# A four-layer scan, FFT and attention kernel: sums moved into PSUM, PSUM banks asked for one at a time, and background steps ordered by the due times of the scan

## The chip, the cores and the metric

The kernel runs on one core of one Trainium2 chip. Its time is the device time of one launch in microseconds (us), and the median of several runs is given. One more execution was recorded by the hardware profiler, with every instruction of the five engines and every DMA. PE is the matrix engine, DVE the vector engine, ACT the scalar engine, POOL the GpSimd engine, and SP the engine that issues all DMAs here. PEld is the loading of matmul weights.

## The reference, cut to what matters

Four images of 96 channels and 64 x 64 pixels (L = 4096 tokens) go through four layers. Nearly all of the time is the first layer's selective scan, in four directions k with 192 channels and 16 states each:

```python
# layer 0, for each image b: LN, projection to xi and z, depthwise 3x3 conv, SiLU
xs = stack of xi in 4 orders: rows, columns, both reversed      # [b, 4, 192, L]
dts_r, Bs, Cs = split(einsum('bkdl,kcd->bkcl', xs, x_proj_w))   # 6 + 16 + 16 rows
dt = softplus(einsum('bkrl,kdr->bkdl', dts_r, dt_projs_w) + dt_bias)
h[t] = h[t-1] * exp(dt[t] * A) + dt[t] * B[t] * x[t]            # 16 states per channel
y[t] = sum over the 16 states of h[t] * C[t]
y = y + Ds * xs
ysum = the 4 directions' y, put back in row order and added     # [b, 192, L]
t = x + (layernorm(ysum) * silu(z)) @ out_proj.T
x = t + gelu(layernorm(t) @ mlp_w1.T + b1) @ mlp_w2.T + b2
# layer 1: x + scale * out_proj(layernorm(scan in 2 directions, 1 state) * silu(z)), on group-normed x
# layer 2: x + FFT filter over the tokens; x + FFN quantized to 8-bit floats
# layer 3: x + linear attention (no softmax); x + FFN quantized in the same way
```

## The kernel before

**The scan as a stream of 1536 units.** The foreground is layer 0's scan. A step g is one image, one direction and one quarter of the tokens (4 x 4 x 4 = 64 steps). A step has 24 units, and a unit is 32 channels x 4 states on the 128 partitions by 1024 tokens. Unit i needs four operations: on ACT the *decay* h = exp(dt * A) into one of two PSUM tiles (`decays`, L1438), on POOL the *source* w = u * bb, with u = dt * x (`sources`, L1459), on DVE the scan itself and then the product w = h * cc with C (`recurs`, L1470). PE then sums the 4 states of two units with the matrix `sel` into the PSUM tile `py` (`gathers`, L1504). For every twelfth unit the product with C is made on POOL instead (`side`, L1495). The decay of unit i waits until the product of unit i-2 has freed its PSUM tile. When `py` holds a block (32 x 2 x 2 rows by 512 tokens, eight units), `collects` (L1525) takes it out: for k = 0 ACT copies it to Y in SBUF, for the other directions ACT copies it to `yt` and POOL adds `yt` to Y.

**Preludes.** Before each step, `preludes` (L1340) loads xi, makes xd, dt and u with matmuls, ACT and POOL, and stores dt and u to DRAM. `loads_du` and `loads_bc` bring them back, spread over the partitions.

**Background.** All the rest runs beside the scan: `front` (LN, projection, conv, L438) of the images 1 to 3, then `rest` of each image: `tail` (L609: `gate` adds the D term, normalizes and gates; `group` makes the projection, the MLP and the residuals), `l1`, `l2_front`, `l2_middle`, `back` with `ffn` (L1060). `front` of image 0 comes before the scan. What is left of image 3's `rest` comes after the last scan, with mode `wide`: more workers, five more PSUM banks, and POOL's share of that work on DVE.

**Who sets the order.** The order on each engine is written by a planner when the program is built (`Work`, L62). Every piece of work is a Python generator that yields `on(engine, events, banks, took, table)` before each step. The planner keeps a clock for each engine and takes, again and again, the step that could start first (`choose`, L153). A step's `ready` is 0.25 us after the end of what it needs. A step that would need a change of the activation table is ranked 0.8 us later. A background step on ACT is passed over if the next decay is ready while it would run, save for its last 1.0 us (`LEAD`):

```python
if lead is not None and t is not self.lead and s < lead < s + took - self.LEAD:
    continue
```

Only the thread that asks first may take PSUM banks, and it waits until all of them are free. On the chip every engine then runs its own list strictly in that order and waits on semaphores, so the planned times matter only through the order. Most lines of the profile name a helper: L212 is every matmul, L216 every ACT copy, L227 every ACT activation, L239 every DVE and POOL operation, L260 loads, L264 stores. So operations are told apart by their tiles.

Of the kernel before, what the change touches and what calls it, by code (L numbers as in the profile page):

```python
# [34 lines left out]
    ("l1cb", 1), ("l1A", 2), ("l1D", 2), ("l1og", 1), ("l1ob", 1), ("l1sc", 1),  # L35
# [14 lines left out]
def on(engine, *events, banks=0, took=0.7, table=None):  # L50

    return engine, events, banks, took, table
# [9 lines left out]
class Work:  # L62
# [3 lines left out]
    LEAD = 1.0  # L66

    def __init__(self):
        self.at = dict(pe=0.0, act=0.0, dve=0.0, pool=0.0, sp=0.0)
        self.link = 0.0  # L70
        self.live, self.events, self.free = [], {}, {}
        self.me = self.lead = self.table = None
        self.pools = {}
        self.held = {}

# [68 lines left out]
    def ready(self, t):  # L144
        r = t.end + (self.GAP if t.ask[0] else 0.0)
        for k in t.ask[1]:
            e = k() if callable(k) else self.events.get(k)
            if e is None:
                return None
            r = max(r, e + self.GAP)  # L150
        return r

    def choose(self):  # L153
        lead = self.ready(self.lead) if self.lead and not self.lead.done else None
        first, cands = None, []
        for t in self.live:
            r = self.ready(t)
            if r is None:
                continue
            cands.append((r, t))  # L160
            if t.ask[2] and (first is None or r < first[0]):
                first = r, t
        best = None
        for r, t in cands:
            e, _, n, took, table = t.ask
            if n:
                if t is not first[1] or len(self.free) < n:
                    continue
                r = max(r, sorted(self.free.values())[n - 1])
            s = max(r, self.at[e]) if e else r  # L170
            key = s
            if e == "act":
                if table and table != self.table:
                    key += 0.8
                if lead is not None and t is not self.lead and s < lead < s + took - self.LEAD:
                    continue
            if best is None or (key, t.rank) < best[0]:
                best = (key, t.rank), s, t
        return best
# [22 lines left out]
def tile_hybrid(ctx: ExitStack, tc: tile.TileContext, I: dict, out: bass.AP):  # L202
# [98 lines left out]
    eye = load_const("eye", [C, C])  # L301
# [10 lines left out]
    def setup():  # L312
# [6 lines left out]
        for j in range(3):  # L319
            ve.reduce_sum(dsum[:, j : j + 1], V("Ds", j=4 * j, n=4), axis=mybir.AxisListType.X)  # L320
        ve.reduce_sum(dsum[0:C, 3:4], V("l1D", C, n=2), axis=mybir.AxisListType.X)
# [7 lines left out]
    centd = const.tile([C, C], F32, name="centd")  # L329

# [4 lines left out]
    PREP = 1262  # L335
# [102 lines left out]
    def front(b):  # L438
# [102 lines left out]
        for part in (1, 0):  # L541
# [6 lines left out]
            def conv(q):  # L548
                def job(t):
                    xi = wt(wk, 128, "xi", t)  # L550
                    early = b == 0 and (t == 0 if part else q < 2)
                    if early:
                        yield from taps(xi, xp, 8 * q, V("cw", j=9 * part, n=9))
                        pc = xi
                    else:
                        (pc,) = yield on("pe", banks=1)
# [52 lines left out]
    def tail(b, stat):  # L609
# [12 lines left out]
        def gate(c):  # L622
            y = ys[c]

            def job(t):
                s3 = wt(wk, 128, "s3", t, (3, HC))
                yield on("sp")
                load_packed(s3, xi_d[b][0], c)
                yield on("act", took=2.1)
                for j in range(3):  # L630
                    act(s3[:, j], s3[:, j], AF.Copy, scale=dsum[:, j : j + 1])
# [4 lines left out]
                e2, name = spare()  # L636
                yield on(name)
                e2.tensor_add(y, y, s3)
# [28 lines left out]
        def group(g):  # L667
# [3 lines left out]
            def job(t):  # L671
# [15 lines left out]
                ps = yield on("pe", banks=3)  # L687
                for f in range(3):
                    mm(ps[f], lhsT=m1[:, f * 128 : f * 128 + 128], rhs=hn, start=True, stop=True)
                yield on("act", took=2.2, table=AF.Gelu)  # L690
                for f in range(3):
                    act(s3[:, f], ps[f], AF.Gelu, bias=bias[:, f : f + 1])
                drop(*ps)
                (po,) = yield on("pe", banks=1)
                for f in range(3):
                    mm(po[0:C], lhsT=m2[:, f], rhs=s3[:, f], start=(f == 0), stop=(f == 2))
                yield on("dve")
                ve.scalar_tensor_tensor(x, po[0:C], V("mb2", C), x, ALU.add, ALU.add)
                ve.bn_stats(stat[:, g, :], x)
                drop(po)  # L700
# [14 lines left out]
    def l1_weights(wp):  # L715
        yield on("sp")
        gavg, w_in, w_out = parcel(wp, "rl1", I["r_l1"], 0, [(C, C), (C, DI), (C, C)])
        (dtc,) = parcel(wp, "pl1", prep, 387, [(C + 1, 2 * (C + 4))])
        return gavg, w_in, w_out, dtc.rearrange("p (k c) -> p k c", k=2)

    def l1(b, stat, pp, big):
# [37 lines left out]
        def edges():  # L759
# [5 lines left out]
            po_.memset(big[C : C + 1], 1.0)  # L765
            po_.memset(u[C : C + 1], 1.0)
# [66 lines left out]
        def piece(n):  # L833
# [4 lines left out]
            def job(t):  # L838
# [59 lines left out]
                pc, pv = yield on("pe", banks=2)  # L898
# [3 lines left out]
                yield on("act")  # L902
                act(a, pc[0:C], AF.Square)
                yield on("pe")
# [3 lines left out]
                rstd(a, pv[0:C])  # L908
                drop(pv)
                yield on("dve")  # L910
                ve.scalar_tensor_tensor(a, pc[0:C], V("l1og", C), a, ALU.mult, ALU.mult)
                drop(pc)
# [3 lines left out]
                mm(po[0:C], lhsT=w_out, rhs=a, start=True, stop=True)  # L916
                yield on("dve")
                ve.scalar_tensor_tensor(x, po[0:C], V("l1sc", C), x, ALU.mult, ALU.add)
# [13 lines left out]
    def l2f_weights(wp):  # L932
        yield on("sp")
        mf1, rij, imp = parcel(wp, "rl2", I["r_l2f"], 0, [(128, 128), (128, DI), (128, DI)])
        (w1,) = parcel(wp, "pl2", prep, 587, [(C + 1, DI)])
# [124 lines left out]
    def ffn(x, rs, buf, lay, wk, t):  # L1060
# [5 lines left out]
        pc, pv = yield on("pe", banks=2)  # L1066
        mm(pc[0:C], lhsT=cent, rhs=x, start=True, stop=True)
        yield on("act")
        act(rs, pc[0:C], AF.Square)
        yield on("pe")  # L1070
        mm(pv[0:C], lhsT=avg, rhs=rs, start=True, stop=True)
        yield on("act", took=1.4, table=LN_EXP)
        rstd(rs, pv[0:C])
        drop(pv)
        yield on("dve")
        ve.tensor_tensor(xq, pc[0:C], rs, ALU.mult, saturate=False)
        drop(pc)
# [32 lines left out]
    def back_weights(wp):  # L1110
        yield on("sp")
        mi2, wff, mask = parcel(wp, "rbk", I["r_back"], 0, [(128, 64), (C, C), (C, C)])
        w2, wqt, wkv, vb = parcel(wp, "pbk", prep, 779, [(C, 2 * C), (C, C + 1), (C + 1, 2 * C), (C, 2)])
        return w2.rearrange("p (h c) -> p h c", h=2), vb, mi2, wqt, wkv, wff, mask

    def back(b):
# [4 lines left out]
        yield on("pool")  # L1121
        po_.memset(y0[C : C + 1], 1.0)
# [109 lines left out]
    def prepare():  # L1232
# [5 lines left out]
        w1 = o[0 : C + 1, 587:779]  # L1238
        w2 = o[0:C, 779:971].rearrange("p (h c) -> p h c", h=2)
        wqt, wkv, vb = o[0:C, 971:1068], o[0 : C + 1, 1068:1260], o[0:C, 1260:1262]  # L1240
# [4 lines left out]
        wq = wp.tile([C, C], F32, name="wq")  # L1245
# [15 lines left out]
        get(wq, I["l3_wq"])  # L1261
        (pb,) = yield on("pe", banks=1)
# [18 lines left out]
        yield on("dve")  # L1281
        ve.tensor_mul(sc, sc, bn[:, 0, :])
# [57 lines left out]
    def preludes():  # L1340
        ck, dp = fg["ck"], fg["dp"]
        for g, (b, k, s, c) in enumerate(steps):
# [40 lines left out]
            act(dtu[:, 0], dtu[:, 0], AF.Ln, bias=one)  # L1383
            yield on("pool")
# [53 lines left out]
    def decays():  # L1438
        for i in range(NU + 2):
            if i >= 2:  # L1440
                yield on("act", ("scan" if (i - 2) % SIDE == SIDE - 1 else "C", i - 2), *([("dt", 6 * place(i)[0] + 2 * place(i)[1] + place(i)[3])] if i < NU else []), took=1.3, table=LN_EXP)
# [7 lines left out]
            else:  # L1449
                g, j, q, p, n = place(i)  # L1450
                yield on("act", ("dt", 6 * g + 2 * j + p), took=1.3, table=LN_EXP)
# [7 lines left out]
    def sources():  # L1459
        for i in range(NU):  # L1460
# [4 lines left out]
            yield on("pool", *need)  # L1465
# [4 lines left out]
    def recurs():  # L1470
        for i in range(NU):
# [5 lines left out]
            yield on("dve", *need)  # L1477
            if i % UNITS == 0 and s == 0:
# [25 lines left out]
    def gathers():  # L1504

        for i in range(1, NU, 2):
            g, j, q, p, n = place(i)
            block = 3 * g + j
            yield on("pe", ("C", i), *([("py", block - 1)] if q == 0 and block else []))
            if q == 0:  # L1510
                live["py"] = fg["py"].tile([128, HC], F32, tag="py", name="py")
            for p in range(2):
                w = live["w"].pop(i - 1 + p)
                for f in range(2):
                    r = p * 64 + f * 32
                    o = live["py"][r : r + 32]
                    if steps[g][1] % 2:
# [4 lines left out]
                    mm(o, lhsT=sel4, rhs=v, start=(q == 0), stop=(q == 3))  # L1522
            post("g", i // 2)

    def collects():  # L1525

        for block in range(3 * NS_):
            g, j = divmod(block, 3)
            b, k, s, c = steps[g]
            yield on("act", ("g", 4 * block + 3), took=1.3)  # L1530
            py = live["py"]
            if k == 0 and s == 0 and j == 0:
                live["Y"] = fg["yp"].tile([128, 3, 2048], F32, tag="Y", name="Y")
            Y = live["Y"]
            if k % 2:
                yv = Y[:, j].rearrange("p (r w) -> p r w", w=WW)[:, :, 16 * c : 16 * c + 16]
            else:
                yv = Y[:, j, c * HC : (c + 1) * HC]
            if k == 0:
                copy(yv, py)  # L1540
                post("py", block)
            else:
                t = fg["ck"].tile([128, HC], F32, tag="yt", name="yt", bufs=1)
                copy(t, py)
                post("py", block)
                o = yv
                if k == 2 and straight(b, c):
                    yield on("pool", ("tail", b))
                    o = last["y"][:, j]
                else:  # L1550
                    yield on("pool")
                po_.tensor_add(o, yv, t.rearrange("p (r w) -> p r w", w=16) if k % 2 else t)
# [3 lines left out]
            elif j == 2 and k == 2:  # L1556
                yield on("sp")
                cs = slice(c * HC, (c + 1) * HC)
                put(y_d[b][:, :, cs], Y[:, :, cs])
# [11 lines left out]
    with tc.manual_schedule():  # L1571
# [15 lines left out]
        ts = [wk_.add(f(), 0) for f in (preludes, collects, gathers, side, sources)]  # L1587
# [28 lines left out]
def _constants():  # L1616
# [12 lines left out]
    for k1 in range(64):  # L1629
# [11 lines left out]
        sel4=np.repeat(np.eye(32), 4, axis=0), eye=np.eye(C),  # L1641
# [4 lines left out]
def _layout(a):  # L1646
# [39 lines left out]
    put("l1og", q["out_norm_w"]); put("l1ob", q["out_norm_b"]); put("l1sc", q["scale_w"].reshape(C))  # L1686
# [46 lines left out]
    def packed_columns(*parts):  # L1733
# [12 lines left out]
        r_l1=packed_columns(k["c_gavg"], d.pop("l1_inT"), d.pop("l1_outT")),  # L1746
# [25 lines left out]
```

## Time and profile before

| what | value |
|---|---|
| three runs | 6716.26, 6720.3, 6737.51 us; median 6720.3 |
| profiled execution: time, span | 6725.84 us, 6724.1 us |
| before the first scan | 0 to 142.7 us |
| from the first scan's start to the last scan's end | 142.7 to 6171.0 us, 6028.3 us long |
| in it, busy: DVE, POOL, PE, ACT | 5579.2, 4972.1, 4528.7, 3896.1 us |
| after the last scan | 6171.0 to 6724.1 us, 553.1 us long |
| in it, busy: PE, ACT, DVE, POOL | 429.7, 273.7, 212.6, 14.9 us |
| granted PE clock: before, during, after the scan | 0.96, 0.84, 0.82 |
| ACT table loads | 239 of 1283 ns |
| POOL: adds of `yt` to Y | 141 + 3, 186.5 us |
| POOL: adds of the D term in `gate` | 30, 103.1 us |
| POOL: fills of single rows with 1.0 | 12, 43.0 us |

Read it like this: the time is the sum of three stretches that follow each other. In the middle one, which is nine tenths of the whole, DVE has 5579 us of work and 449 us without work. The page's own chain of work that ended last reaches back over the last stretch and a few pieces before it, and so it says little on the middle one; that has to be read from the waits of DVE.

### The profile page before, as it was taken

What the parts mean: (1) busy time and instruction counts of PE and PEld (TensorE: products, weight loads), DVE (VectorE), ACT (ScalarE), POOL (GpSimd) and SP (SyncE); (2) the same over time, 40 slices, a digit from 0 to 9 for tenths busy, and PEclk for the clock granted to TensorE, in tenths of its full rate; (3) what the DMA queues carried; (4) which work ended last, traced back from release to release, by engine and by line L of the source; (5) the groups of instructions that cost most, each with busy time, mean ns of one, the idle gap of its engine ahead of it and who ended that gap; (6) DMA issues with size and microseconds to landing.
All of it is one profiled execution on the core that took longest, in us unless ns stands there. A gap on an engine that the chain in (4) does not pass through costs nothing. (4 is left out here: it accounts for less than half of the span.)

```text
span 6724.1 us, 54939 instructions
## 1 busy us (share of the span) xinstructions
PE 5070.8 (75%) x15240; PEld 1576.7 (23%) x15240; DVE 5827.8 (87%) x3933; ACT 4222.9 (63%) x6376; POOL 5010.5 (75%) x2319
## 2 busy tenths in 40 slices
PE   7687878766866888767767888767866888767788
PEld 2121212111211332211211232212211332212263
DVE  3899899899999999989989999999999999987613
ACT  3566566555765567766665567876765557765535
POOL 2788788888798788887798788888798778885000
PEclk9688999777868998877879899878877999878788
DMA  4556565656555775555555685566554685562551
GB/s 147 175 173 195 154 202 169 187 173 183 165 183 153 225 265 172 168 169 175 179 172 159 192 295 176 167 189 185 165 184 151 207 283 161 161 178 91 154 158 34
DMA packets 530050, 1188.80 MB, mean 177 GB/s; under 512 B 87970, under 2 KB 161135, under 8 KB 529744
## 3 DMA queue, kind: packets, MB, share of 16 engines
q1 hardware_dynamic: 529744, 1185.30, 57.1%
q8 instruction: 121, 1.98, 0.1%
q14 instruction: 185, 1.52, 0.1%
HBM read 937.50 MB, written 247.59 MB: 176 GB/s over the span
## 5 line engine op out<-in xcount | busy, mean ns | idle before, releaser
L239 POOL TENSOR_TENSOR w<-u,bb 128x1024 f32<-128x1024 f32 x1536 | 3617.0, 2376 | 849.3 <-PE py L212 741.7
L239 DVE TENSOR_TENSOR_SCAN h<-h,state,w 128x1024 f32<-128x1024 f32 x1056 | 2480.2, 2349 | 173.5 <-ACT h L227 112.0
L212 PE MATMUL py<-w,sel 128*32 128x512 f32 x6144 | 1823.9, 971 | 710.1 <-DVE w L239 524.7
L227 ACT ACTIVATE h<-dt,negA 128x1024 f32<-128x1024 f32 x1536 | 1728.6, 1126 | 431.0 <-DVE w L239 309.9
L239 DVE TENSOR_TENSOR w<-h,cc 128x1024 f32<-128x1024 f32 x1408 | 1722.2, 1223 | 107.7 <-DVE h L239 2.7
L239 DVE TENSOR_TENSOR_SCAN h<-h,w 128x1024 f32<-128x1024 f32 x352 | 805.1, 2287 | 103.6 <-ACT h L227 93.7
L216 ACT COPY state<-h 128x1 f32<-128x1 f32 x1056 | 165.8, 157 | 858.7 <-DVE w L239 855.5
L212 PEld LDWEIGHTS py<-w,sel 128*32 128x32 f32 x6144 | 184.8, 117 | 1793.7 <-DVE w L239 1017.7
L239 POOL TENSOR_TENSOR w<-w,cc 128x1024 f32<-128x1024 f32 x128 | 301.3, 2354 | 89.5 <-ACT state L216 53.4
L212 PE MATMUL bm<-xp,dg 128*128 128x512 f32 x792 | 362.3, 605 | 1.3 <-ACT xi L227 1.0
L212 PE MATMUL bm<-xi,xw 128*128 128x512 f32 x384 | 237.6, 769 | 145.6 <-DMA xi<-xi_d 137.1
L227 ACT ACTIVATE dtu<-bm 128x512 f32<-128x512 f32 x384 | 209.4, 600 | 79.2 <-PE bm L212 76.5
L239 POOL TENSOR_TENSOR dtu<-dtu 128x1536 f32<-128x1536 f32 x64 | 221.4, 3459 | 47.6 <-ACT state L216 30.9
L212 PE MATMUL bm<-xd,dtw 64*128 64x512 f32 x384 | 226.2, 675 | 32.2 <-ACT xd L227 5.7
L239 DVE TENSOR_TENSOR_SCAN w<-h,state,w 128x1024 f32<-128x1024 f32 x96 | 224.7, 2341 | 6.4 <-ACT state L216 4.4
L239 POOL MEMSET y<- 1x4096 f32 x4 | 14.1, 3513 | 289.8 <-DMA g_d<-o 289.6
L239 POOL TENSOR_TENSOR dtu<-dtu,xi 128x1536 f32<-128x1536 f32 x64 | 222.5, 3477 | 0.2
L212 PE MATMUL bm<-big,dg 96*96 96x512 f32 x450 | 214.8, 624 | 5.1 <-ACT u L227 3.5
L239 POOL TENSOR_TENSOR Y<-Y,yt 128x512 f32<-128x512 f32 x141 | 182.7, 1296 | 33.2 <-ACT yt L216 21.4
L212 PEld LDWEIGHTS bm<-xp,dg 128*128 128x128 f32 x792 | 145.1, 190 | 263.0 <-issue 248.4
L212 PE MATMUL bm<-x,cent 96*96 96x512 f32 x272 | 158.1, 680 | 53.1 <-DMA x<-in_x 18.5
L239 DVE TENSOR_TENSOR h<-bm,rs 96x512 fp8e5<-96x512 f32 x54 | 36.7, 679 | 162.2 <-ACT rs L227 155.2
(310 smaller groups left out, 7049.5 us busy)
## 6 DMA issues: line engine op xcount, KB each, us to landing
u<-dd SPq DMA_DIRECT2D x384, 512.0 KB
dt<-dd SPq DMA_DIRECT2D x384, 512.0 KB
bb<-bc SPq DMA_DIRECT2D x256, 512.0 KB
cc<-bc SPq DMA_DIRECT2D x256, 512.0 KB
dd<-dtu SPq DMA_DIRECT2D x256, 384.0 KB
xi<-xi_d SPq DMA_DIRECT2D x256, 192.0 KB
f_d<-fo SPq DMA_DIRECT2D x64, 384.0 KB
a<-f_d SPq DMA_DIRECT2D x64, 384.0 KB
```

The lines of the kernel that those rows point to most:

```text
L212: return nc.tensor.matmul(o, lhsT=lhsT, rhs=rhs, **kw)
L216: return nc.scalar.copy(o, i, **kw)
L227: return nc.scalar.activation(o, i, func, **kw)
L239: return f(o, *a, **kw)
```

## The change

The diff has four parts.

**Sums in PSUM.** `gathers` starts each block of `py` with a full 128 x 128 matmul: for k = 0 the D term, from the raw conv output `xj` and the matrix `diagD` (the sum of the four directions' D on the diagonal), for the other directions the part of Y so far, with a unit matrix. ACT then copies `py` straight to Y; `yt` and POOL's adds are gone. A new thread `convolved` loads `xj` for the 48 blocks with k = 0 (four DMAs each). `gate` loses its load of xi, three ACT scalings and the add. In the MLP (`group`) and in layer 1 (`piece`) the residual enters by a unit matrix, and ACT instead of DVE takes the sum out; layer 1's scale is multiplied into its weights beforehand.

**Single-bank requests.** Where a step asked for two or three banks, it asks for one. For that, centred values are copied by ACT from PSUM to SBUF (`dt` in layer 1, `xc` in `ffn`), the reciprocal deviation stays in PSUM, and the MLP's three results are taken out one by one with the bias and go through one Gelu of 1536 columns.

**Due times.** A step of the scan on ACT or POOL carries its unit's number. The planner keeps the pace of the scan and works out by when the unit is due. Until then the step may be ranked up to 0.8 us later, and the next decay blocks background on ACT only from its due time on. A change of table counts with 1.28 us for each load, there and back. Two steps of one thread on the same engine no longer have 0.25 us between them.

**Smaller edits.** Rows of ones come by DMA instead of POOL's fills. In the first image, six of the eight conv pieces of the last part wait until the first prelude has got to its logarithm (`begun`).

```diff
 class Work:
+    UNIT, MARGIN, YIELD, AGE = 3.6, 0.5, 0.8, 0
+    def latest(self, unit, took):
+        i, t = self.pace
+        return t + (unit - i) * self.UNIT - took - self.MARGIN
...
     def ready(self, t):
-        r = t.end + (self.GAP if t.ask[0] else 0.0)
+        r = t.end + (self.GAP if t.ask[0] and t.ask[0] != t.last else 0.0)
...
     def choose(self):
+        if lead is not None and self.lead.ask[5] is not None:
+            lead = max(lead, self.latest(self.lead.ask[5], self.lead.ask[3]))
...
+            if unit is not None:
+                key = max(s, min(s + self.YIELD, self.latest(unit, took)))
             if e == "act":
-                if table and table != self.table:
-                    key += 0.8
-                if lead is not None and t is not self.lead and s < lead < s + took - self.LEAD:
+                if table:
+                    took += 1.28 * ((table != self.table) + (table != LN_EXP))
+                if lead is not None and t is not self.lead and s < lead < s + took - self.LEAD - self.AGE * (s - r):
                     continue
...
     def front(b):
+                    if b == 0 and part == 0 and q >= 2:
+                        yield on(None, ("begun",))
...
         def gate(c):
-                load_packed(s3, xi_d[b][0], c)
-                yield on("act", took=2.1)
-                for j in range(3):
-                    act(s3[:, j], s3[:, j], AF.Copy, scale=dsum[:, j : j + 1])
...
-                e2.tensor_add(y, y, s3)
...
         def group(g):
-                ps = yield on("pe", banks=3)
                 for f in range(3):
-                    mm(ps[f], lhsT=m1[:, f * 128 : f * 128 + 128], rhs=hn, start=True, stop=True)
-                yield on("act", took=2.2, table=AF.Gelu)
-                for f in range(3):
-                    act(s3[:, f], ps[f], AF.Gelu, bias=bias[:, f : f + 1])
+                    (ph,) = yield on("pe", banks=1)
+                    mm(ph, lhsT=m1[:, f * 128 : f * 128 + 128], rhs=hn, start=True, stop=True)
+                    yield on("act")
+                    act(s3[:, f], ph, AF.Identity, bias=bias[:, f : f + 1])
+                yield on("act", took=1.5, table=AF.Gelu)
+                act(s3, s3, AF.Gelu)
...
+                mm(po[0:C], lhsT=eye, rhs=x, start=False, stop=True)
+                yield on("act")
+                act(x, po[0:C], AF.Identity, bias=V("mb2", C))
                 yield on("dve")
-                ve.scalar_tensor_tensor(x, po[0:C], V("mb2", C), x, ALU.add, ALU.add)
                 ve.bn_stats(stat[:, g, :], x)
...
     def ffn(x, rs, buf, lay, wk, t):
-        pc, pv = yield on("pe", banks=2)
+        (pc,) = yield on("pe", banks=1)
...
+        copy(xc, pc[0:C])
+        drop(pc)
+        (pv,) = yield on("pe", banks=1)
...
-        ve.tensor_tensor(xq, pc[0:C], rs, ALU.mult, saturate=False)
+        ve.tensor_tensor(xq, xc, pv[0:C], ALU.mult, saturate=False)
...
     def gathers():
-            yield on("pe", ("C", i), *([("py", block - 1)] if q == 0 and block else []))
             if q == 0:
+                yield on("pe", *([("py", block - 1)] if block else []), *([] if k else [("xj", block)]))
...
+                if k:
+                    o = py.rearrange("p (r w) -> p r w", w=16) if k % 2 else py
+                    mm(o, lhsT=eye128, rhs=y_part(block), start=True, stop=False)
+                else:
+                    mm(py, lhsT=diagD[:, j], rhs=live["xj"], start=True, stop=False)
+            yield on("pe", ("C", i))
...
     def collects():
-                t = fg["ck"].tile([128, HC], F32, tag="yt", name="yt", bufs=1)
-                copy(t, py)
...
-                po_.tensor_add(o, yv, t.rearrange("p (r w) -> p r w", w=16) if k % 2 else t)
+            copy(o, py.rearrange("p (r w) -> p r w", w=16) if k % 2 else py)
```

Layer 1's `piece` is changed like `ffn` and `group`. Both programs hold 239 table loads.

## The prediction

> **What bounds the kernel now.** I read the page's busy times first: DVE has 5827.8 us of 6724.1, more than any other engine, so the question is where DVE stands. The view by windows, cut at the first and the last scan, gives it: between them (6028.3 us) DVE works 5579.2 and is idle 449.1; after them DVE works only 212.6 of 553.1. The groups then say what a unit costs.
>
> ```profile
> PE 5070.8 (75%) x15240; PEld 1576.7 (23%) x15240; DVE 5827.8 (87%) x3933; ACT 4222.9 (63%) x6376; POOL 5010.5 (75%) x2319
> ```
>
> ```profile
> L239 POOL TENSOR_TENSOR w<-u,bb 128x1024 f32<-128x1024 f32 x1536 | 3617.0, 2376 | 849.3 <-PE py L212 741.7
> L239 DVE TENSOR_TENSOR_SCAN h<-h,state,w 128x1024 f32<-128x1024 f32 x1056 | 2480.2, 2349 | 173.5 <-ACT h L227 112.0
> ...
> L227 ACT ACTIVATE h<-dt,negA 128x1024 f32<-128x1024 f32 x1536 | 1728.6, 1126 | 431.0 <-DVE w L239 309.9
> L239 DVE TENSOR_TENSOR w<-h,cc 128x1024 f32<-128x1024 f32 x1408 | 1722.2, 1223 | 107.7 <-DVE h L239 2.7
> ```
>
> A scan (2.35 us) and its product (1.22) make 3.57 us per unit on DVE, and neither is touched by the change. POOL and ACT wait for the loop (849 and 431 us before these rows), so a lighter POOL is worth nothing by itself. What can be won in the loop is DVE's background work and DVE's waits. The waits of DVE from 150 to 6180 us (columns: total us, times, longest):
>
> ```profile
> DVE h L239 <- ACT h L227: 151.4, 114, 11.8
> DVE h L239 <- ACT state L216: 56.9, 38, 5.7
> DVE a L239 <- POOL a L239: 29.8, 15, 4.5
> DVE h L239 <- POOL w L239: 17.2, 10, 4.1
> DVE y L239 <- ACT bm L227: 16.3, 10, 4.5
> DVE yc L239 <- PE bm L212: 15.7, 7, 4.2
> ```
>
> Of the 449 us, 110 are pieces of at most 0.15 us between a scan and its product, which stay. The other 339 are waits: 230 before scans (nearly all for a late decay on ACT) and 109 before background steps.
>
> **Start: -10 us.** The timeline of ACT from 99 to 122 us:
>
> ```profile
> 100.14 0.69 ACT L227 ACTIVATE xd<-bm,vec 128x512 f32<-128x512 f32 x1 [6.32 <-PE bm L212]
> ...
> 106.34 1.09 ACT L227 ACTIVATE dtu<-bm 128x512 f32<-128x512 f32 x2 [2.89 <-PE bm L212]
> 110.17 1.09 ACT L227 ACTIVATE dtu<-bm 128x512 f32<-128x512 f32 x2 [2.74 <-PE bm L212]
> ...
> 114.00 1.09 ACT L227 ACTIVATE dtu<-bm 128x512 f32<-128x512 f32 x2 [0.32 <-PE bm L212]
> ...
> 117.91 1.57 ACT L227 ACTIVATE dtu<-dtu,one 128x1536 f32<-128x1536 f32 x1
> ```
>
> Between them PE does conv matmuls (5.31 + 2.85 + 2.84 us). With `begun` they come later: the first dtu pair at 100.83 + 1.15 = 102.0, the pairs back to back until 105.3, then table load 1.28, Exp 1.48, Ln 1.57, so Ln ends near 109.7 and not at 119.5. The first scan moves from 142.7 to about 133. The six pieces go into the loop; in the changed order their table loads stand singly between decays, and one such interval is 1.28 + 0.69 + 1.28 = 3.25 us, below the 3.5 from which waits grow (below), so I cost them at nothing; uncovered, six would cost about 6 us.
>
> **DVE's work in the loop: -36 us.** The residual adds of MLP and layer 1 leave DVE: 28 x 0.734 = 20.6 and 24 x 0.729 = 17.5 us there. Added: three scalings for diagD and one of weights, 2. ACT takes the sums out instead.
>
> Here a rule speaks against the change. The Trainium skill, "ScalarE: Activation LUTs", Rules for kernel authors, says that simple adds and products belong on VectorE, not on ScalarE. For this shape the trace differs: an ACT copy out of PSUM takes 0.58 us, DVE's form 0.73. By the rule the move loses some us; by the rows it takes 38 off the bound engine and puts it on one with slack.
>
> A second rule speaks for a larger gain than I take. "SBUF — State Buffer", Who interferes with whom: a VectorE instruction with two SBUF inputs shares a port with GpSimd's reads under an exclusive lock; with one, it doesn't. POOL loses 186.5 us of Y adds, half of the 103.1 of D adds, and 43.0 of fills, 281 in all. If each could hold DVE up, that would be worth up to 281. But scan and product read h in PSUM and one operand in SBUF, and their times are tight (2326/2349/2379 and 1156/1225/1247 ns min/median/max), so nothing holds them. Only small steps show it: 24 of `a<-a,vec,cc` take 1.80 in the loop against 0.72 at best. With 6% less POOL that is 1.5 us. I take nothing.
>
> **Waits before background steps: -51 us.** Here I join the trace with the order of the instructions as built (it has no times). I count how many decays stand before a producer on ACT and how many scans before its user on DVE; the difference is the distance. With distance -1 the mean idle before the DVE step is 0.489 us (143 steps), with 0 it is 0.081 (95). The changed order has 40 and 215. So 69.9 + 7.7 becomes 19.6 + 17.4. Steps whose latest producer is PE: 27.3 us for 192 steps, with the same means 21.0 for 168. POOL's and the rest 6.9, then 2.6. The sum goes from 111.8 to 60.6.
>
> **Waits before scans: -6 us, the open term.** ACT's background grows by 96 copies (64 xc, 32 dt, 0.58 each), 32 copies and 32 Identities for residuals (0.58, 0.68) and 32 wide Gelu (1.48, the time of a 1536-column Square), less 48 scalings (31.1 us): 112 us, some 92 in the loop. Table loads are 239 in both orders. Three parts:
> - By the background between two decays, in durations of rows: below 2.8 us the mean wait of the next scan is 0.092 (1285 intervals), to 3.5 it is 0.242 (137), above 0.686 (114). The new order has 1290, 107, 139: 230 becomes 240.
> - ACT steps close behind PE (same count of distance, 2) go from 170 to 331, the mean ACT idle before them 0.87 us against 0.34 at distance 3: 87 us more idle. ACT has 2132 us idle in the loop. An interval with one such step shows 0.153 us of scan wait, one with none 0.146; finer classes with both features give +9.
> - ACT waits 143.4 us for the prelude's first matmul, because PE waits 137 for xi; 33 us of scan waits lie behind this. The new order has xi's loads less than two units ahead of the matmul 12 times and not 64: -25.
>
> ```profile
> ACT xd L227 <- PE bm L212: 143.4, 46, 7.7
> ```
>
> Bounds: at best half of the 230 goes (-115), because due times and counted table loads keep ACT free for decays; at worst the 87 and the 92 reach the scans whole (+179). I take -6, since the classes come from this trace. Waits for dt's DMA (43 us before scans, behind the long runs of stores of the transposed xi on SP) stay: eight such runs in both orders. What the change adds to SP's queue are 192 loads of xj, less 64 of xi in `gate`; each waits for the block before, and behind it stand loads of dt and u, but these are still issued early (lowest twentieth for dt 3.0 units ahead before and 2.8 after, for u 2.5 and 1.5, and POOL runs up to six units ahead).
>
> **PE** gets 192 full matmuls for py and 64 for residuals. By the conv row (792 records of half a matmul, 362.3 us: 0.915 each) that is 234 us. In the loop PE works 4529 of 6028, and py's first matmul waits for the same copy as before, now ahead of the product. No cost but what the second part above counts. Uncovered, 0.9 us per block of eight units would be 170.
>
> **After the last scan: +9 us.** The chain there is 60% PE. In the new order 18 more matmuls stand behind the last scan (12 for residuals, 6 of two more MLP groups): 18 x 0.915 x 0.6 = 10; ACT 41 steps more, 16% of the chain, 3. POOL's last Y add (1.26) and DVE's D add (1.76) with a handover go: -4.
>
> **Sum.** -10 - 36 - 51 - 6 + 9 = -94: 6725.8 becomes 6632. The profiled execution lies 5.5 us over the median of the runs, so I forecast 6626.
>
> **The rivals.**
> - *Due times keep decays punctual.* Half of the scan waits go, -115 in place of -6: 6517. For it: 55 of the 230 stand behind table loads in an unbroken run on ACT. Against it: the built order has more long intervals, not fewer.
> - *Waits only change their name.* DVE steps are placed later, but the idle time shows up before the next scan, so the -51 falls: -10 - 36 + 9 - 6 = -43, 6677. For it: a third of the waits are ones that no order of DVE can help. Against it: 0.489 against 0.081.
> - *ACT becomes late (slower).* The added 179 us of ACT work and idle time sit between decays, and of them a share reaches the scans. -94 turns into a loss once the share is over 94/179 = 53%. At two thirds: +25, 6745. For it: 139 long intervals. Against it: in the trace one close step costs the scan nothing.
>
> **How the numbers follow.** About 0.3% is what a measurement of this kernel can tell from no change, 6700 to 6740. Chances: forecast 0.5 (6580 to 6680), punctual decays 0.2, renamed waits 0.18 (a few of them above 6700), ACT late 0.12. So faster 0.84, same 0.08, slower 0.08. The range reaches from the better half of the second case to the edge of the third: 6530 to 6705.
>
> **What would show it.** First scan at 132 to 135 us. DVE's busy time near 5790. `yt` and POOL's adds gone, POOL near 4730. In the loop, waits of background steps on ACT fall to half or less, waits of h for ACT stay near 210. ACT's xd waits far below 143, other ACT waits for PE longer. Last stretch 555 to 570. If the scan waits fall under 150 or rise over 300, the open term was wrong, and with it the forecast.

## The result and the profile after

The changed kernel takes 6662.2 us in the median of 6 runs (6648.8 to 6666.7). The kernel before took 6721.6 on the same chip (6 runs). The ratio is 0.9906, with a 95% interval of 0.9890 to 0.9921: faster by 59 us. The profiled execution of the changed kernel has a span of 6647.0 us, 77 less than the one of before. It lies 13 us under the median of its runs, and the one of before lies 4 us over its own; that is why the profiles differ by 77 and the medians by 59. In what follows the ratios leave out the few executions that were far longer at a lower granted clock (13833 us at 0.378 in run 2, 6916 at 0.698 in run 4), while the medians in us include them.

The busy times of the page, then the groups that carry a unit of the scan (in a group, after the first bar: busy us and mean ns of one; after the second: the engine's idle time before them, and what ended most of it):

```profile
PE 5289.4 (80%) x15752; PEld 1653.6 (25%) x15752; DVE 5807.2 (87%) x3872; ACT 4308.0 (65%) x6520; POOL 4740.5 (71%) x2148
```

```profile
L254 POOL TENSOR_TENSOR w<-u,bb 128x1024 f32<-128x1024 f32 x1536 | 3607.6, 2374 | 907.0 <-PE py L227 785.3
L254 DVE TENSOR_TENSOR_SCAN h<-h,state,w 128x1024 f32<-128x1024 f32 x1056 | 2480.8, 2349 | 177.5 <-ACT h L242 89.2
...
L242 ACT ACTIVATE h<-dt,negA 128x1024 f32<-128x1024 f32 x1536 | 1727.7, 1125 | 428.5 <-DVE w L254 304.1
L254 DVE TENSOR_TENSOR w<-h,cc 128x1024 f32<-128x1024 f32 x1408 | 1721.8, 1223 | 109.5 <-DVE h L254 3.2
```

Scan and product cost what they cost. POOL lost 270 us of work, and waits 58 us longer before `w<-u,bb`. PE has 219 us more, ACT 85, DVE only 21 less. The waits of DVE from 150 to 6080 us (total us, times, longest):

```profile
DVE h L254 <- ACT h L242: 119.2, 101, 14.8
DVE h L254 <- ACT state L231: 76.6, 40, 12.2
DVE h L254 <- POOL w L254: 47.4, 37, 2.5
DVE yc L254 <- ACT bm L242: 3.5, 5, 1.1
```

Of the waits before background steps (`a`, `y`, `yc` in the view of before) almost nothing is left. In the waits before scans, decays are less often to blame, ACT's copies of the state and POOL's `w` more often.

The granted PE clock in the loop also differs: 0.84 before, 0.88 after. It does not carry the gain: it is 0.85 in run 1 below, which gains as much, and 0.86 in run 2, which gains nothing.

The table splits each profiled execution. "Background" and "scan" are DVE's idle times of over 0.15 us in the loop, by what comes after them. "Held" is explained with run 4.

| kernel | first scan at | loop | after it | DVE work in the loop | idle: background | idle: scan | held |
|---|---|---|---|---|---|---|---|
| before | 142.7 | 6028.3 | 553.1 | 5579.2 | 107.7 | 228.2 | 48.3 |
| after | 133.3 | 5948.3 | 565.4 | 5568.2 | 19.2 | 247.0 | 84.1 |
| 1 order alone | 170.0 | 5933.1 | 552.4 | 5596.1 | 16.8 | 209.3 | 85.2 |
| 2 sums alone | 143.4 | 5996.6 | 564.1 | 5548.9 | 97.2 | 239.6 | 51.3 |
| 3 no `begun` | 158.3 | 5945.7 | 563.9 | 5565.8 | 26.7 | 241.0 | 83.1 |
| 4 one SBUF operand | 131.8 | 5902.6 | 562.6 | 5504.8 | 25.0 | 259.3 | 19.0 |
| 5 no due times | 132.3 | 6057.4 | 622.1 | 5536.0 | 187.3 | 213.3 | 59.5 |
| 6 order and `begun` | 133.7 | 5966.9 | 554.8 | 5582.5 | 31.2 | 246.2 | 70.1 |
| 7 as 6, one SBUF operand | 134.9 | 5940.7 | 557.6 | 5547.6 | 21.6 | 264.1 | 31.1 |
| 8 sources undated | 132.8 | 5916.6 | 623.4 | 5551.7 | 22.7 | 227.0 | 76.9 |
| 9 old charge | 131.2 | 6225.2 | 558.0 | 5597.8 | 124.1 | 394.7 | 97.0 |
| 10 as 4, no Y sums | 132.5 | 5903.8 | 574.9 | 5505.4 | 26.2 | 259.3 | 22.2 |
| 11 as 9, one SBUF operand | 131.0 | 6136.7 | 556.3 | 5524.2 | 104.0 | 401.0 | 22.1 |
| 12 two SBUF operands more | 133.7 | 5946.4 | 556.7 | 5555.3 | 15.5 | 258.3 | 68.9 |

### The profile page after: what moved, and what is told of

The parts are those of the page before. It is cut to its first block, busy times and chain, and to the rows that moved or that the text cites. A ratio compares the mean times of both kernels' runs of the same rounds, so it can differ in the third digit from the quotient of the medians.

```text
span 6647.0 us, 55955 instructions
## 1 busy us (share of the span) xinstructions
PE 5289.4 (80%) x15752; PEld 1653.6 (25%) x15752; DVE 5807.2 (87%) x3872; ACT 4308.0 (65%) x6520; POOL 4740.5 (71%) x2148
## 5 line engine op out<-in xcount | busy, mean ns | idle before, releaser
L227 PE MATMUL py<-w,sel 128*32 128x512 f32 x6144 | 1847.9, 930 | 511.3 <-DVE w L254 381.7
L227 PE MATMUL py<-Y,eye 128*128 128x512 f32 x288 | 166.2, 660 | 42.6 <-ACT Y L231 39.8
L242 ACT ACTIVATE bm<-bm,eps 96x512 f32<-96x512 f32 (+1 forms) x210 | 135.7, 646 | 64.7 <-PE bm L227 64.4
L227 PE MATMUL bm<-x,cent 96*96 96x512 f32 x278 | 148.9, 628 | 19.6 <-DMA x<-in_x 5.5
```

The source lines that it names most:

```text
L227: return nc.tensor.matmul(o, lhsT=lhsT, rhs=rhs, **kw)
L242: return nc.scalar.activation(o, i, func, **kw)
```

## The experiments

The theory after reading the result: the gain comes from the order, which puts DVE's background steps behind their producers, and the sums bring little. The rival: the sums bring it. A second question came from the DVE rows: 52 adds left DVE's part of the loop, and its work there fell by 11 us only.

**Runs 1 and 2: the two halves of the change.** Run 1 is the kernel before with the new planner rules:

```diff
-        r = t.end + (self.GAP if t.ask[0] else 0.0)
+        r = t.end + (self.GAP if t.ask[0] and t.ask[0] != t.last else 0.0)
...
+            lead = max(lead, self.latest(self.lead.ask[5], self.lead.ask[3]))
...
+                key = max(s, min(s + self.YIELD, self.latest(unit, took)))
...
-            yield on("pool", *need)
+            yield on("pool", *need, took=2.4, unit=i)
```

> The kernel before with the planner's new rules alone (handover charge only between engines, due times, table loads counted on ACT, PSUM banks out of turn); no sums in PSUM, no `begun`. If the order is what gained: waits of DVE before background steps fall from 109 us to 20 to 40, waits before scans rise by about 18, DVE's work in the loop stays at 5579, so about 6660 us. If the sums gained and the order only renames waits: idle time of DVE in the loop stays near 440, 6710 to 6725 us. First scan at 142 to 143 us in both.

The new rules hold one that the section on the change does not name: a thread may take a free PSUM bank out of turn. Its patience is 0, so this happens only when the thread is ready at the same moment as the first asker; no run takes it alone.

Run 2 is the changed kernel with `ready` and `choose` of before, and without `begun`.

> The changed kernel with the planner's old rules and without `begun`: parts of Y, the D term and the residuals in PSUM sums, single banks. If the order is what gained in the change: DVE's waits before background steps stay near 100 us, its work in the loop falls by 36 at most, the stretch after the last scan grows by some 10, so 6690 to 6700 us. If the sums gained: 6665 to 6680 us. If more steps on ACT and PE make the decays late under the old rules: over 6722 us.

Measured: the order alone 6657.8 us, ratio 0.9903 (0.9887 to 0.9920). The sums alone 6713.0, ratio 0.9996 (0.9984 to 1.0008). So in the kernel as built the order is the whole gain. DVE's waits in run 1 (175 to 6100 us) and in run 2 (150 to 6140 us):

```profile
DVE h L254 <- ACT h L242: 98.5, 84, 4.4
DVE h L254 <- POOL w L254: 60.2, 44, 4.5
DVE h L254 <- ACT state L231: 39.1, 29, 3.4
DVE yc L254 <- PE bm L227: 7.7, 3, 3.3
```

```profile
DVE h L248 <- ACT h L236: 160.3, 105, 12.9
DVE h L248 <- ACT state L225: 53.6, 27, 6.2
DVE a L248 <- POOL a L248: 32.4, 22, 3.4
DVE yc L248 <- PE bm L221: 18.7, 10, 3.3
```

Run 2 still has the old picture (`a`, `yc`), run 1 the new one. Two details were missed. The first scan of run 1 came at 170 us and not at 142. And run 2 gained less than the 20 to 30 us expected: its loop is 32 us shorter, but its last stretch 11 longer, and the medians show nothing.

**Run 3: without `begun`,** two edits of `front` and `preludes` taken back.

```diff
-                    if b == 0 and part == 0 and q >= 2:
-                        yield on(None, ("begun",))
...
-            if g == 0:
-                post("begun")
```

> The changed kernel without `begun`. If the start was worth what the first scan moved by: first scan at about 142.5 us and not 133.3, the loop as long as before, 6671 us. If the six conv pieces that `begun` puts into the loop cost there what they free at the start: the loop is 6 to 9 us shorter, 6662 us.

Measured 6669.1 us, ratio 0.9925 (0.9913 to 0.9937), against 0.9906 with it. The loop is as long as before the edit (5945.7 and 5948.3), so the pieces cost nothing there. The first scan is at 158, not at 142.5: without `begun` the new rules put more ahead of it than the old ones.

**Run 4: who took DVE's saving?** The rows of layer 1's two scaling steps in the changed kernel's loop (busy us, mean ns):

```profile
L254 DVE SCALAR_TENSOR_TENSOR a<-a,vec,cc 96x512 f32<-96x512 f32 x24 | 67.5, 2816 | 1.7 <-DMA cc<-z_d 1.7
...
L254 DVE SCALAR_TENSOR_TENSOR a<-dt,vec,bm 96x512 f32<-96x512 f32 x24 | 17.3, 724 | 0.0
...
L254 DVE TENSOR_TENSOR gm<-mv,gm 96x1 f32<-96x1 f32 x3 | 8.8, 2926 | 0.1
```

Two of these rows before:

```profile
L239 DVE SCALAR_TENSOR_TENSOR a<-a,vec,cc 96x512 f32<-96x512 f32 x24 | 43.2, 1799 | 0.0
...
L239 DVE TENSOR_TENSOR gm<-mv,gm 96x1 f32<-96x1 f32 x3 | 0.5, 156 | 0.1
```

Two steps of one kind and shape take 0.72 and 2.82 us; the slow one reads `a` and `cc` from SBUF, the fast one `dt` from SBUF and `bm` from PSUM. Before, the slow one took 1.80 and `gm` 0.16. The timeline (start us, length us) shows what the slow ones wait for, DVE first, then POOL:

```profile
3508.80 2.29 DVE L254 TENSOR_TENSOR_SCAN h<-h,w 128x1024 f32<-128x1024 f32 x1
3511.00 6.84 DVE L254 SCALAR_TENSOR_TENSOR a<-a,vec,cc 96x512 f32<-96x512 f32 x1
3517.77 1.21 DVE L254 TENSOR_TENSOR w<-h,cc 128x1024 f32<-128x1024 f32 x1
```

```profile
3505.71 11.59 POOL L254 TENSOR_TENSOR w<-u,bb 128x1024 f32<-128x1024 f32 x5
```

POOL's five products end at 3517.30, and the DVE step ends at 3517.84, 0.54 us later. This holds in all the long cases: the step ends 0.55 us after the end of a POOL instruction, of the one that ran when it began or of one of the next three. I call such a step held, and count what it lasts beyond the shortest of its shape in any of these traces, where that is over 0.4 us. Run 4 lets the first scaling write to PSUM, so that the second reads one operand from SBUF, and makes the same of the group norm's small steps:

```diff
-                ve.scalar_tensor_tensor(a, dt, V("l1og", C), pv[0:C], ALU.mult, ALU.mult)
-                drop(pv)
+                ve.scalar_tensor_tensor(pv[0:C], dt, V("l1og", C), pv[0:C], ALU.mult, ALU.mult)
                 yield on("dve")
-                ve.scalar_tensor_tensor(a, a, V("l1ob", C), yf, ALU.add, ALU.mult)
+                ve.scalar_tensor_tensor(a, pv[0:C], V("l1ob", C), yf, ALU.add, ALU.mult)
+                drop(pv)
...
-            ve.tensor_sub(gm[:, 1:2], mv[:, 0:1], gm[:, 0:1])
-            ve.tensor_mul(gm[:, 1:2], gm[:, 1:2], gm[:, 1:2])
-            ve.tensor_add(gm[:, 2:3], gm[:, 1:2], mv[:, 1:2])
+            ve.tensor_sub(gm[:, 1:2], mv[:, 0:1], pg[0:C, 0:1])
+            ve.tensor_scalar(gm[:, 2:3], gm[:, 1:2], gm[:, 1:2], mv[:, 1:2], ALU.mult, ALU.add)
```

> The changed kernel with the first layer 1 scaling writing to PSUM, so that the step a<-a,vec,cc reads one operand from SBUF and not two, and the group norm's three steps of one column as two of one SBUF operand each. If a DVE step with two SBUF operands is held until POOL's running instruction has ended: the 24 steps in the loop take 0.72 us and not 2.82, the small gm steps 0.15 and not 2.4, DVE's work in the loop falls by about 65 us, and since DVE is the bound the time falls by 50 to 65, to about 6605 us. If the long durations come from something else (DMA traffic, the shape): they stay near 2.8 us and the time at 6662. If DVE then waits for decays instead: durations fall but the waits before scans rise by as much, about 6650.

Measured 6601.0 us, ratio 0.9822 (0.9808 to 0.9837): the fastest kernel of this study, 56 us under the changed one by the ratios (0.0084 of 6715). The same two steps in its loop:

```profile
L254 DVE SCALAR_TENSOR_TENSOR a<-bm,vec,cc 96x512 f32<-96x512 f32 x24 | 17.5, 734 | 1.2 <-DMA cc<-z_d 1.1
L254 DVE SCALAR_TENSOR_TENSOR bm<-dt,vec,bm 96x512 f32<-96x512 f32 x24 | 17.5, 734 | 0.3 <-ACT bm L242 0.2
```

Both take 0.73 us. Held time falls by 65 us, DVE's work by 63, the time by 56; waits before scans take back 12.

**Run 5: no due times.** What in the new rules makes the order?

```diff
-                yield on("act", ..., took=1.3, table=LN_EXP, unit=min(i, NU - 1))
+                yield on("act", ..., took=1.3, table=LN_EXP)
...
-                yield on("act", ("dt", 6 * g + 2 * j + p), took=1.3, table=LN_EXP, unit=i)
+                yield on("act", ("dt", 6 * g + 2 * j + p), took=1.3, table=LN_EXP)
...
-            yield on("pool", *need, took=2.4, unit=i)
+            yield on("pool", *need, took=2.4)
```

> The changed kernel with no unit given for decays and sources, so that no due time enters the planner; all else as changed. The order as built then has 140 ACT producers a decay too late for their DVE step (distance -1 or -2), against 40 in the changed kernel and 143 before. If the due times carry the gain of the order: DVE's waits before background steps return to 80 to 100 us, and the time to about 6725 us. If the other rules (handover charge, table loads, banks) carry it: 6650 to 6670 us.

Measured 6816.4 us, ratio 1.0143 (1.0119 to 1.0168): the direction was right and the size far off. Background steps of DVE wait again for ACT (133 to 6190 us):

```profile
DVE h L254 <- ACT h L242: 104.7, 45, 44.6
DVE h L254 <- POOL w L254: 93.8, 29, 27.8
DVE h L254 <- ACT bm L242: 84.7, 16, 30.0
DVE h L254 <- ACT state L231: 54.1, 26, 16.8
DVE y L254 <- ACT bm L242: 48.4, 9, 18.8
```

The third row is not a scan but `ffn`'s first step h, which waits up to 30 us. Joined with the order as built, 23 steps stand at distance -2 (two decays too late), and they alone wait 131.5 us; no step stood there before. More work is also left for the last stretch (622 us).

**Runs 6 and 7: no sums, with and without the held steps.** Run 6 is run 1 with `begun` (the edit of run 3 the other way). Run 7 adds the edit of run 4, with `pc` in place of `dt`.

```diff
-                ve.scalar_tensor_tensor(a, pc[0:C], V("l1og", C), a, ALU.mult, ALU.mult)
-                drop(pc)
+                ve.scalar_tensor_tensor(pc[0:C], pc[0:C], V("l1og", C), a, ALU.mult, ALU.mult)
                 yield on("dve")
-                ve.scalar_tensor_tensor(a, a, V("l1ob", C), yf, ALU.add, ALU.mult)
+                ve.scalar_tensor_tensor(a, pc[0:C], V("l1ob", C), yf, ALU.add, ALU.mult)
+                drop(pc)
```

> The kernel before with the planner's new rules and `begun`, no sums in PSUM. In the run of the order alone the first scan came at 170 us; with `begun` it should come at 133. If the sums are worth nothing or cost some time in the new order: loop near 5935 us, last stretch 552, so 6620 us, well below the changed kernel. If the sums gain once the order is mended: over 6662 us. If `begun` only moves work into the loop: 6645 to 6655 us.

> As the run with the new order and `begun` and no sums, and the layer 1 scaling through PSUM and the group norm's steps with one SBUF operand. If held DVE steps cost what they last beyond their undisturbed time (51 us of them in the run of the order alone): about 6570 us. If the freed time turns into waits before scans: within 15 us of the run without it.

Run 6: 6651.5 us, ratio 0.9896 (0.9872 to 0.9920). Against run 1 the first scan is 36 us earlier and the loop 34 longer, so here `begun` only moved work, as its third expectation said. The changed kernel, which has the sums as well, is no faster (0.9906). Run 7: 6626.2, ratio 0.9860 (0.9836 to 0.9884), a gain of 24, not 51. I had taken the 51 us from run 1; in run 6 the edited steps are held for less, and held time falls by 39, DVE's work by 35. Waits before scans take back 18. Three masks of `kvacc`, 5.6 us each in the mean, were not edited and stay held.

With most of the held time gone, the sums do pay: run 7 (without) 0.9860, run 4 (with) 0.9822, some 26 us. The two intervals just touch, but the loops of the profiles agree: run 4's is 38 us shorter, with 43 us less work of DVE.

**Run 8: sources without a due time,** the third edit of run 5 alone.

> The changed kernel with due times for decays but none for POOL's products w = u*B. If the due time puts these products too late: waits of scans for POOL w fall from 47 us to the 17 of before, and the time to about 6635 us. If these waits come from something else (a later dtu, ACT's state copies): they stay at 40 to 50 us and the time within 10 us of 6662.

Measured 6661.1 us, ratio 0.9914 (0.9887 to 0.9941). The theory fell: scans wait 56 us for POOL's `w`, not 17. The loop is 32 us shorter, but 58 us more are left for the last stretch.

**Runs 9 and 11: the old charge for a handover,** alone and with the edit of run 4.

```diff
-        r = t.end + (self.GAP if t.ask[0] and t.ask[0] != t.last else 0.0)
+        r = t.end + (self.GAP if t.ask[0] else 0.0)
```

> The changed kernel with the handover charge of before (0.25 us before every request, not only where a thread changes its engine); due times and all else stay. In the changed kernel 47 us of scan waits for POOL w stand behind pairs of layer 1 products that POOL runs back to back. If the new charge makes these pairs: waits for POOL w fall to about 20 and the time to about 6640 us. If the new charge is also a part of what puts DVE's background steps later: their waits rise from 19 to 30 or 40 us, and the sum is near 6660.

> The old handover charge and the layer 1 scaling through PSUM together, in the changed kernel. If POOL's pairs cost 25 us and the held steps 60: 6575 us. If the charge is worth nothing: 6601 us as with the scaling alone.

Run 9: 6904.2 us, ratio 1.0281 (1.0262 to 1.0299). I had expected a small gain, and it is the slowest of all. POOL's `w` is as late as before, so the charge doesn't explain that wait; instead decays come late (133 to 6350 us):

```profile
DVE h L254 <- ACT h L242: 354.1, 176, 44.9
DVE h L254 <- POOL w L254: 40.4, 31, 2.1
DVE yc L254 <- PE bm L227: 34.8, 13, 4.9
```

Run 11: 6822.6 us, ratio 1.0166 (1.0149 to 1.0183). One SBUF operand is worth 77 us here, where held time falls by 75.

So in the changed kernel due times and the new charge work only together: with both 0.9906, due times without the charge 1.0281, the charge without due times 1.0143; with neither (run 2, which also lacks the other rules and `begun`) 0.9996. Why decays come late in run 9 was not followed further.

**Run 10: run 4 without the sums of Y and D.** `gathers` and `collects` are those of before, `gate` scales and adds the D term again, `convolved` and `diagD` are gone.

```diff
-        ts = [wk_.add(f(), 0) for f in (preludes, collects, convolved, gathers, side, sources)]
+        ts = [wk_.add(f(), 0) for f in (preludes, collects, gathers, side, sources)]
...
+                load_packed(s3, xi_d[b][0], c)
+                yield on("act", took=2.1)
+                for j in range(3):
+                    act(s3[:, j], s3[:, j], AF.Copy, scale=dsum[:, j : j + 1])
...
+                e2.tensor_add(y, y, s3)
...
-                    mm(o, lhsT=sel4, rhs=v, start=False, stop=(q == 3))
+                    mm(o, lhsT=sel4, rhs=v, start=(q == 0), stop=(q == 3))
...
+                po_.tensor_add(o, yv, t.rearrange("p (r w) -> p r w", w=16) if k % 2 else t)
```

> The changed kernel with the layer 1 scaling through PSUM (6601 us in its run), and the Y and D sums undone: Y and D added by POOL and DVE as before, the residual sums, single banks and the order kept. If a lighter POOL is worth nothing by itself and the residuals alone bring what the sums bring: 6595 to 6610 us, POOL's busy time near 5000. If the sums of Y bring it: 6625 us, as in the run without any sums.

Measured 6610.3 us, ratio 0.9852 (0.9838 to 0.9867). POOL is busy for 4967.6 us, 228 more than in run 4, and the loop is the same to 1.2 us. By the ratios the sums of Y and D are worth 20 us, by the profiles 14, and 12 of these lie after the last scan. So what the sums bring in the loop comes from the residuals, or from the single-bank requests, which no run takes apart from them; run 10's 42 us less work of DVE than run 7's, near the 38 of the residual adds, speak for the residuals.

**Run 12: a second step with two SBUF operands.**

```diff
-                rstd(pv[0:C], pv[0:C])
+                rstd(a, pv[0:C])
+                drop(pv)
                 yield on("dve")
-                ve.scalar_tensor_tensor(a, dt, V("l1og", C), pv[0:C], ALU.mult, ALU.mult)
-                drop(pv)
+                ve.scalar_tensor_tensor(a, dt, V("l1og", C), a, ALU.mult, ALU.mult)
```

> The changed kernel with layer 1's rstd written to SBUF, so that a second step (a<-dt,vec,bm, 0.72 us, 24 in the loop) also reads two operands from SBUF. If such a step is held until POOL's instruction has ended: this step takes 2 to 3 us, DVE's work in the loop grows by 30 to 55 us and the time to 6690 to 6715 us. If only the other step is slow for a reason of its own: it stays at 0.72 us and the time at 6662.

```profile
L254 DVE SCALAR_TENSOR_TENSOR a<-dt,vec,a 96x512 f32<-96x512 f32 x24 | 59.7, 2499 | 0.0
...
L254 DVE SCALAR_TENSOR_TENSOR a<-a,vec,cc 96x512 f32<-96x512 f32 x24 | 17.4, 733 | 0.0
```

The first step is held now, from 0.72 to 2.50 us, so operands decide it and not the step. But the second is held no more, the two take 77.1 us together where they took 84.8, and the time stays (6644.2, ratio 0.9907, 0.9892 to 0.9922). Both expectations missed this. In the trace the second step always begins where POOL's instruction has 0.11 us or less to run, or POOL is idle. Presumably the wait of the first has brought it there; no run shows that.

## Why the prediction was right or wrong

The forecast was -94 us between profiled executions, and they show -77. The median was forecast at 6626 us and came to 6662, inside the range. Of these 36 us, 17 are in the steps below; the other 19 come from taking the profiled execution to lie 5.5 us over the median, where that of the changed kernel lay 13 under it. By its own steps:

- **Start, -10: -9.4.** First scan at 133.3, forecast 133. The dtu pieces stand back to back, as worked out, and Ln ends at 112.4, not 109.7, because the first xd comes at 102.9:

```profile
102.88 0.69 ACT L242 ACTIVATE xd<-bm,vec 128x512 f32<-128x512 f32 x1 [13.05 <-PE bm L227]
...
104.78 3.18 ACT L242 ACTIVATE dtu<-bm 128x512 f32<-128x512 f32 x6 [1.21 <-PE bm L227]
```

  That six pieces cost nothing in the loop held in this order (run 3), not in the one without sums (runs 1 and 6).

- **DVE's work in the loop, -36: -11.0. This step failed, at "I take nothing" for the shared port.** The adds did go: 20.6 and 17.5 us, as worked out, and without held time the steps of the loop are 41 us shorter in sum. But held time rose from 48.3 to 84.1 us: 25 for `a<-a,vec,cc`, 20 for `gm`. That is 36 us, the whole of the step. (The busy time shows -11 and not -5, since it counts overlapping ends of steps once.) The prediction had the row (1.80 us against 0.72) and the rule of the Trainium skill, "SBUF — State Buffer", Who interferes with whom (a VectorE step with two SBUF inputs and a GpSimd instruction that reads SBUF exclude each other for the whole instruction, and who comes first decides). It scaled the row by POOL's busy time, 6% less. What counts is not POOL's share of the span but whether it runs, and goes on running, when the step begins: 20 of the 24 such steps in the loop met a running POOL before, 21 after. But before, 3 of them sat through more than one POOL instruction, after 7 did, up to 7.98 us. The rise comes with the order: held time is 85.2 us in run 1, which has the order alone, and 51.3 in run 2, which has the sums alone. Which of its rules does it stays open.

- **Waits before background steps, -51: -88.** The direction and the cause were right, the size was too small. The counted distances are those of the run, but not the means that I put on them: 40 steps at distance -1 wait 1.9 us, not 19.6; 215 at distance 0 wait 9.7, not 17.4; those behind PE 6.3, not 21.0. A class's mean from the old order does not carry over to a new one. What makes the same distance cheaper was not tried.

- **Waits before scans, -6: +19** (228.2 to 247.0), inside the bounds of -115 and +179 and near the guess. It is made up differently: decays fell from 154 to 122, state copies rose from 55 to 77, POOL's `w` from 17 to 47. POOL's part the prediction did not have. 32 of its 47 us stand where POOL had worked without a pause and, of its last 14 instructions at most, four or more were products of layer 1 or of a prelude. Two theories of what makes them (runs 8 and 9) fell; it stays open, but it comes with the new rules: 65 us in run 1, 17 in run 2. xi's loads are earlier, as counted:

```profile
ACT xd L242 <- PE bm L227: 83.2, 37, 6.5
```

  ACT waits for PE in all for 713 us (150 to 6080 us), against 714: xd's waits fell by 60, the others rose by 59, not by 87.

- **After the last scan, +9: +12.3.** Run 10 puts the gain from Y and D there at 12, not 4, so the residuals and the single banks cost some 24, not 13.

Together: -9.4 - 11.0 - 88.5 + 18.8 + 12.3, and 0.7 of small pieces, make -77. That this is near -94 is in part luck: DVE's work and the scan waits each came out 25 us worse than forecast, the background waits 37 us better. "Waits only change their name" came true for 19 us of 88. "Punctual decays" holds for ACT's decays by a fifth, and others came in their place. "ACT late" did not come: the waits of scans for decays and state copies are 209 before and 199 after. And "a lighter POOL is worth nothing by itself" held to 1.2 us in the loop (run 10).

## What to carry to other kernels

When an engine is the bound, compare the mean and the shortest duration of each of its small shapes, and take every step that is longer than its shortest apart: here an output moved to PSUM, without a single instruction more, was worth as much as the whole change. Rules of an order should be tried together as well as alone: here each of two without the other lost 1.4 and 2.8%, and both together gained 0.9%. Distances counted in a built order told here where waits would fall, but not how long they would be.

## What the hardware showed that I had not expected

A DVE step with two operands from SBUF that begins while POOL runs ends 0.54 to 0.56 us (once 0.61) after POOL's instruction for 96x512, and 0.013 to 0.016 after it for 96x1. DVE can be passed over, which "who comes first decides" does not cover: POOL began two or three further instructions while a step of 0.72 us took 6.84 to 7.98. Where POOL was idle, 11 such steps of the changed kernel took 0.74 to 0.75. A product `w` of POOL that stood behind such a DVE step took 2.80 to 2.92 us in place of 2.35. Two SBUF tensors are not the only case: a DVE scaling of one SBUF tensor by one number per partition (`rl<-rl,gm`, 96x192), which takes 0.32 us after the last scan, took 1.68 to 3.51 in the loop of run 4 and ended 0.11 to 0.12 us after a POOL instruction.
